# One layer on one core: experts' gate and up products with stationary weights, scatters without mutual order, and part of the experts' transfers on GpSimd's queue

## The chip, the core and the metric

The kernel runs on one core of a Trainium2 chip. The core has TensorE (PE) for matrix products, VectorE (DVE) and ScalarE (ACT) for elementwise work, GpSimd (POOL), and SyncE (SP), which issues most of the DMAs. Each engine executes its own instructions in order and waits on semaphores for the others. DMAs issued from SP and from POOL are carried by the same 16 DMA engines.

The metric is the device time of one execution in microseconds (us), here the median of several runs. Lower is better. Before the change it is 2605.57 us (three runs, 2600.91 to 2608.23).

## The reference

The layer takes 512 rows of width 512 (`x`) and a context of 8192 rows. It adds three blocks to `x` one after the other: cross attention with 16 heads of width 64, a state-space block with an MLP, and a mixture of 16 experts with a shared expert. The parts that the change touches are the projections at the start of the attention and the experts:

```python
x = x + _L0_xattn_ref(_layernorm(x), ctx, ctx, Wq, bq, Wk, bk, Wv, bv, Wo, bo)
...
logits = jnp.einsum('btc,ec->bte', x, router_w)          # x is the layernormed row
top_vals, top_idx = jax.lax.top_k(logits, 2)
gates = jax.nn.sigmoid(top_vals)
w_full = zeros((N, 16)).at[arange(N)[:, None], sel].add(gates)
gu = jnp.einsum('nc,ech->neh', xf, gate_up_w)            # 16 experts, 512 -> 2 x 512
gate, up = jnp.split(gu, 2, axis=-1)
h = jax.nn.silu(gate) * up
out_all = jnp.einsum('neh,ehc->nec', h, down_w)          # 512 -> 512
moe = jnp.einsum('ne,nec->nc', w_full, out_all)
shared = silu(x @ shared_gate.T) * (x @ shared_up.T) @ shared_down.T
x = x + moe + shared
```

Every row goes to its two best experts only, so the kernel gathers rows by expert.

## The kernel before

**Numbers in pairs.** All large products run in fp16 with a high and a low half of each operand and three matmuls per product (high by high, high by low, low by high), summed in fp32 in PSUM. A weight that comes from DRAM as fp32 is therefore split: ACT writes the high half, DVE the low half.

**Start (pass 0 of the attention).** `filler` (L426) is a generator that emits the key, value and query projections. For head pairs 0 and 1 it goes over 16 chunks of 512 context rows. For each chunk, `ctx_first` (L224) loads two pieces of 512 KB, splits them and stores the halves; `kproj_units` (L247) and `vproj_units` (L267) multiply them by the weights. `stage_w` (L168) loads a weight and `split_w` splits it; `load_w` does both at once. The staging tiles of Wk for pair 1 and of Wv share the tag `p32` and its three buffers with the context pieces `cf` (L229). `first_norm` (L186) normalises `x` and transposes it, `qproj` (L203) makes the queries; both are emitted after chunk 0 (L483 to L486). `smax_units` (L287) is the pass that finds each row's maximum: in pass 0 a unit is four matmuls into four PSUM banks (L300), four ACT copies (L305) and one DVE maximum. These units are queued in the list `side`, and `pump` (L429) hands one out after every fourth projection unit. PE's order in this part is the order in which `filler` emits, by hand; the other engines' order is set by the scheduler of the framework.

**Middle.** From about 250 us to 2230 us the attention's main loop and then the state-space block run. The change does not touch them.

**Experts (`tail`, L633).** Here the framework schedules all engines. The shared expert (`ffn`, L955, with the weights `rsg`, `rsu`, `rsd`) runs for the two halves of the rows. Its weights use the tag `wpm`, which has five buffers. Meanwhile DVE works out, for each row, the two slots (`sg`) in a table `xd_d` in DRAM, which holds 128 rows for each of 23 groups: 16 experts and 7 overflow groups. Eight indirect DMAs on POOL's queue scatter the rows into the table (L1199 to L1204), 128 rows of 2 KB each. The framework sees eight writes to one tensor and makes each wait for the one before.

Then `moe` (L1259) goes over 18 groups: 16 experts and 2 overflow groups. The other five run only in a branch that depends on a count. For each group k:

- `pieces` (L1084) loads four gate-and-up pieces and two down pieces of 512 KB each, in fp32, through the six buffers `wef` on SP's queue, and splits them: into `we` (18 buffers) and into `wpm` (the five that the shared expert uses too).
- `moe_in` (L1206) loads the group's rows `xd` from the table on SP's queue (three buffers), transposes them on PE in eight steps, and ACT copies the result to `xk`.
- `moe_up` (L1217) multiplies with the *rows* stationary: 24 matmuls, each with a 128x128 block of `xk` loaded into the array and 512 columns of weights moving. Row r of PSUM belongs to token r. ACT and DVE make silu(gate) times up and split it into `mgg`.
- `moe_turn` (L1237) transposes `mgg` on PE in eight steps so that features lie on partitions, and DVE copies the result to `mgT`. It is called in the middle of the *next* group's `moe_up`.
- `moe_down` (L1246) runs 12 matmuls with `mgT` stationary and 512 columns of the down weights moving. ACT copies the result to `myo`, and SP stores it to `y_d` (L1257).

At the end POOL gathers each row's two results from `y_d` (L1285), DVE adds them to `x_sb` with the gates (L1289), and SP stores the output.

Of the kernel before, what the change touches and what calls it, by code (L numbers as in the profile page):

```python
# [8 lines left out]
F16 = mybir.dt.float16  # L9
# [7 lines left out]
P = 128  # L17
# [7 lines left out]
WS = 16.0  # L25
# [13 lines left out]
def perceiver_layer(ctx: ExitStack, tc: tile.TileContext, a: dict, out: bass.AP):  # L39
# [120 lines left out]
    bq_sb = sb1.tile([P, NPAIR], F32, name="bq_sb")  # L160
    bk_sb = sb1.tile([P, NPAIR], F32, name="bk_sb")
    bv_sb = L.tile([P, NPAIR], F32, name="bv_sb")
    nc.sync.dma_start(bq_sb, a["bq"])
    nc.sync.dma_start(bk_sb, a["bk"])
    nc.sync.dma_start(bv_sb, a["bv"])
    nc.vector.tensor_scalar(bk_sb, bk_sb, WS, None, ALU.mult)

    def stage_w(src, n, tag, stage=("wst", 1), bufs=2):  # L168
        st = sb2.tile([P, NC4, n], F32, name=f"wst_{tag}", tag=stage[0], bufs=stage[1])
        nc.sync.dma_start(st, src)  # L170
        return lambda: split_w(st, n, tag, bufs)

# [7 lines left out]
    def load_w(*x, **k):  # L180
        return stage_w(*x, **k)()
# [244 lines left out]
    def filler():  # L426
        side = []

        def pump():  # L429
            while side:  # L430
                u = next(side[0], None)
                if u is not None:
                    yield u
                    break
                side.pop(0)

        def pass_weights(g):
            pr = (2 * g, 2 * g + 1)
            out = []
            for src, n, tag, bufs in (  # L440
                (a["Wk"][pr[0]], P, "k", 4), (a["Wk"][pr[1]], P, "k", 4), (a["Wv"][g], 256, "v", 2),
                (a["Wq"][pr[0]], P, "q", 2), (a["Wq"][pr[1]], P, "q", 2),
            ):
                w = stage_w(src, n, tag, bufs=bufs)
                yield None
                out.append(w())
            yield out[0:2], out[2], out[3:5]

        nw = None
        for g in range(NPASS):  # L450
            pr = (2 * g, 2 * g + 1)
            if g == 0:
                wk0 = load_w(a["Wk"][0], P, "k", bufs=4)
                nct = ctx_first(0)
                wk = [wk0, load_w(a["Wk"][1], P, "k", ("p32", 3), bufs=4)]
                wv = load_w(a["Wv"][0], 256, "v", ("p32", 3))
                nc.sync.dma_start(x_sb, a["x"])
                wq = [load_w(a["Wq"][p], P, "q", ("t2k", 4)) for p in pr]
            else:
                wk, wv, wq = nw  # L460
                qh = [qproj(p, w) for p, w in zip(pr, wq)]
                yield 2 * 2592
            runm = [None, None]
            ks = [[None] * NCH for _ in pr]
            for c in range(NCH):
                if c == NCH - 7 and g < NPASS - 1:
                    nws = pass_weights(g + 1)
                if c >= NCH - 7 and g < NPASS - 1:
                    nw = next(nws, None) or nw
                ct = nct  # L470
                nxt = g * NCH + c + 1
                if nxt < NPASS * NCH:
                    nct = ctx_first(nxt) if nxt < NCH else ctx_load(nxt % NCH)
                gens = [kproj_units(p, c, ct, wk[i], ks[i]) for i, p in enumerate(pr)]
                gens += [vproj_units(g, c, ct, wv, j) for j in range(2)]
                k = 0
                for n, gen in enumerate(gens):
                    for u in gen:
                        yield u
                        k += 1  # L480
                        if k % (2 if g else 4) == 0 or len(side) > 2:
                            yield from pump()
                if g == 0 and c == 0:  # L483
                    first_norm()
                    qh = [qproj(p, w) for p, w in zip(pr, wq)]
                    yield 2 * 2592  # L486
                if c == 2:
                    for p, q in zip(pr, qh):
                        qplace(p, *q)
                side += [smax_units(c, i, qh[i][0], ks[i][c], runm, g == 0) for i in range(2)]  # L490
            side += [maxrow_units(p, i, runm) for i, p in enumerate(pr)]
            if g == NPASS - 1:
                while side:
                    yield from pump()
                    yield LAST / 10
            passes[0] = g + 1
# [136 lines left out]
def tail(tc, a, out, const, scr, ident, x_sb, mlp_d, oT, y_d, xd_d, psums):  # L633
# [562 lines left out]
    oii = G.tile([P, NOV + 1], I32, name="oii")  # L1196
    nc.vector.tensor_copy(oii, oid)

    for i in range(4):  # L1199
        for j in range(2):  # L1200
            nc.gpsimd.indirect_dma_start(
                out=xd_d[:], out_offset=bass.IndirectOffsetOnAxis(ap=sg[:, j, i : i + 1], axis=0),
                in_=xf[:, i].rearrange("p x d -> p (x d)"), in_offset=None,
            )  # L1204

    def moe_in(k):  # L1206
        xd = g2.tile([P, 2, NC4, P], F16, name="xd", bufs=3)
        nc.sync.dma_start(xd, xd_d[k * P : (k + 1) * P, :].rearrange("t (x d m) -> t x d m", x=2, d=NC4))
        pt = bank_j([P, 2, NC4, P], F16, "pxd")
        for x in range(2):  # L1210
            for d in range(NC4):
                nc.tensor.transpose(pt[:, x, d, :], xd[:, x, d, :], id16)
        xk = g2.tile([P, 2, NC4, P], F16, name="xk", bufs=2)
        nc.scalar.copy(xk, pt)
        return xk

    def moe_up(xk, ws, mid):  # L1217
        pg = bank_j([P, 512], F32, "pmg")
        pu = bank_j([P, 512], F32, "pmu")
        for d in range(NC4):  # L1220
            if d == 2 and mid:
                mid()
            for n, (x, y) in enumerate(((0, 0), (0, 1), (1, 0))):
                for o, ps in ((0, pg), (512, pu)):
                    nc.tensor.matmul(
                        ps, lhsT=xk[:, x, d, :], rhs=ws[d][:, y, o : o + 512],
                        start=d == 0 and n == 0, stop=d == 3 and n == 2,
                    )
        g = F2.tile([P, 512], F32, name="mg", tag="g32", bufs=2)
        nc.scalar.activation(g, pg, AF.Silu, scale=IW)  # L1230
        nc.vector.scalar_tensor_tensor(g, pu, IW, g, ALU.mult, ALU.mult)
        gg = F2.tile([P, 2, 512], F16, name="mgg", tag="gg", bufs=2)
        nc.scalar.copy(gg[:, 0], g)
        nc.vector.tensor_tensor(gg[:, 1], g, gg[:, 0], ALU.subtract)
        return gg

    def moe_turn(gg):  # L1237
        pt = bank_j([P, 2, NC4, P], F16, "pmt")
        for x in range(2):
            for c in range(NC4):  # L1240
                nc.tensor.transpose(pt[:, x, c, :], gg[:, x, c * P : (c + 1) * P], id16)
        gT = g2.tile([P, 2, NC4, P], F16, name="mgT", bufs=2)
        nc.vector.tensor_copy(gT, pt)
        return gT

    def moe_down(k, gT, ws):  # L1246
        py = acc(k % 4)
        for c in range(NC4):
            for n, (x, y) in enumerate(((0, 0), (0, 1), (1, 0))):
                nc.tensor.matmul(  # L1250
                    py, lhsT=gT[:, x, c, :],
                    rhs=ws[4 + c // 2][:, y, (c % 2) * 512 : (c % 2) * 512 + 512],
                    start=c == 0 and n == 0, stop=c == 3 and n == 2,
                )
        yo = g2.tile([P, DM], F32, name="myo", tag="yo", bufs=4)
        nc.scalar.activation(yo, py, AF.Copy, scale=IW)
        nc.sync.dma_start(y_d[k * P : (k + 1) * P, :], yo)  # L1257

    def moe(ks, weights):  # L1259
        xk = moe_in(ks[0])  # L1260
        prev = None
        turned = []
        for k in ks:
            ws = weights(k)
            gg = moe_up(xk, ws, prev and (lambda: turned.append(moe_turn(prev[1]))))
            if k < ks[-1]:
                xk = moe_in(k + 1)
            if prev:
                moe_down(prev[0], turned.pop(), prev[2])
            prev = k, gg, ws  # L1270
        moe_down(prev[0], moe_turn(prev[1]), prev[2])

    regs = [nc.sync.value_load(oii[0:1, k : k + 1], min_val=0, max_val=15) for k in range(NOV)]
    for _ in rs0:
# [87 lines left out]
```

## Time and profile before

| what | us |
|---|---|
| median of three runs | 2605.57 |
| the profiled execution, its own time | 2611.01 |
| its span, first to last instruction | 2609.3 |
| PE busy / DVE busy / ACT busy / POOL busy | 2383.2 / 2062.4 / 1949.2 / 44.3 |

The profile is of one execution. Its span is 1.7 us shorter than its own time, and its time is 5.4 us above the median. A page of the profile gives, for the whole span, the busy time of each engine; further views give the busy time, the TensorE clock that was granted and the DMA rate for chosen stretches, the instructions in order of time, and for each wait the instruction that ended it. PE is busy for 91% of the span, but this is a mean over stages with different limits, and a matmul's recorded duration (380 ns for 512 columns) is longer than its distance to the next one (216 ns), because matmuls overlap.

Where the stages lie: pass 0 of the attention from 0 to about 250 us; main loop and state-space block to about 2230 us; the rest of the MLP and the first half of the shared expert to about 2352 us; the scatters from 2352.8 us to 2387 us, beside the shared expert's second half; 18 groups of experts from 2402 us to 2587 us; gathers and output to 2609 us.

### The profile page before, as it was taken

The numbers are of one execution on the slowest core, as the hardware profiler recorded it, in microseconds if no ns is written. First come the engines' busy times: TensorE is split into PE (matmuls) and PEld (weight loads), VectorE is DVE, ScalarE is ACT, GpSimd is POOL, SyncE is SP. The second block draws the span as 40 slices with busy tenths as digits, with TensorE's granted clock in tenths as the row PEclk, the third lists the DMA queues.
The fourth block names the chain that finished last, engine by engine and source line by source line (L and its number), as shares of the span: only waits on it lengthen the run. The fifth ranks groups of instructions, "written<-read, shape, count | busy, mean of one in ns | idle before, by whom it ended". The sixth has DMA issues, their size and how long they took to land. (4 is left out here: it accounts for less than half of the span.)

```text
span 2609.3 us, 54424 instructions
## 1 busy us (share of the span) xinstructions
PE 2383.2 (91%) x21806; PEld 1676.5 (64%) x21806; DVE 2062.4 (79%) x2403; ACT 1949.2 (75%) x3734; POOL 44.3 (2%) x58
## 2 busy tenths in 40 slices
PE   7999899999999999999999998997877688998895
PEld 3555577776677777767777777995665466665442
DVE  6776588888888888878888778997899999533785
ACT  5787788888788888868888888997776476333784
POOL 2000000000000000000000000000000000001001
PEclk9999999999999999999999999999989899999998
DMA  7974677778687778778877655877510222766896
GB/s 270 312 259 138 231 212 231 229 235 241 199 234 235 226 221 251 226 199 228 236 221 213 175 156 148 207 205 192 159 41 25 97 81 82 260 225 217 293 331 208
DMA packets 353688, 531.43 MB, mean 204 GB/s; under 512 B 25107, under 2 KB 218835, under 8 KB 353301
## 3 DMA queue, kind: packets, MB, share of 16 engines
q1 hardware_dynamic: 352148, 523.69, 65.8%
q0 software_dynamic: 1280, 4.20, 0.5%
q8 instruction: 173, 2.83, 0.5%
q14 instruction: 87, 0.70, 0.1%
HBM read 397.68 MB, written 126.94 MB: 201 GB/s over the span
## 5 line engine op out<-in xcount | busy, mean ns | idle before, releaser
L377 DVE TENSOR_TENSOR phl<-p,phl 128x1024 f16<-128x1024 f32 x512 | 626.7, 1225 | 193.2 <-ACT phl L374 181.0
L372 ACT ACTIVATE p<-pss 128x512 f32<-128x512 f32 x1024 | 597.7, 622 | 114.5 <-PE pss L365 42.2
L305 ACT ACTIVATE sf<-psx 128x512 f16<-128x512 f32 x1024 | 558.5, 625 | 70.9 <-PE psx L300 70.1
L364 PE MATMUL pss<-qhh,k 128*128 128x256 f16 x2048 | 481.0, 275 | 14.3 <-ACT phl L374 12.0
L365 PE MATMUL pss<-qlm,kb 128*128 128x256 f16 x2048 | 479.7, 274 | 0.9 <-DMA kb<-k_d 0.9
L313 DVE TENSOR_TENSOR runm<-runm,sf 128x2048 f16<-128x2048 f16 x240 | 292.3, 1219 | 51.7 <-ACT sf L305 51.5
L394 PE MATMUL po<-v,phl 128*128 128x130 f16 x4096 | 322.7, 220 | 3.9 <-DVE oq L407 3.4
L374 ACT ACTIVATE phl<-pss 128x512 f16<-128x512 f32 x512 | 312.8, 611 | 0.0
L394 PEld LDWEIGHTS <-phl 128*128 128x128 f16 x4096 | 271.0, 98 | 61.6 <-issue 14.8
L275 PE MATMUL psv<-wh_v,ctxc 128*128 128x256 f16 x1024 | 282.0, 275 | 7.3 <-ACT wh_v L176 3.2
L276 PE MATMUL psv<-wl_v,ctxc 128*128 128x256 f16 x1024 | 280.8, 274 | 1.2 <-DVE wl_v L177 1.2
L277 PE MATMUL psv<-wh_v,ctxc 128*128 128x256 f16 x1024 | 280.9, 274 | 0.0
L364 PEld LDWEIGHTS <-k 128*128 128x128 f16 x2048 | 200.9, 98 | 66.0 <-issue 20.0
L365 PEld LDWEIGHTS <-kb 128*128 128x128 f16 x2048 | 201.4, 98 | 53.0 <-issue 14.6
L300 PE MATMUL psx<-khl,qh 64*128 64x512 f16 x1024 | 208.9, 386 | 17.6 <-ACT sf L305 12.2
L922 PE MATMUL py<-hs,ident 128*128 128x256 f32 x512 | 144.0, 437 | 73.5 <-DVE hs L919 73.5
L397 PE MATMUL po<-v,phl 128*128 128x65 f16 x4096 | 208.5, 193 | 2.5 <-DVE phl L377 2.5
L251 PE MATMUL psk<-ctxc,wh_k 128*128 128x512 f16 x512 | 198.0, 387 | 9.9 <-ACT ctxc L234 8.1
L376 DVE CAST phl<-p 128x1024 f16<-128x1024 f32 x256 | 176.0, 687 | 32.2 <-ACT p L372 32.0
L252 PE MATMUL psk<-ctxc,wh_k 128*128 128x512 f16 x512 | 196.3, 383 | 0.8 <-DVE ctxc L235 0.7
L253 PE MATMUL psk<-ctxc,wl_k 128*128 128x512 f16 x512 | 196.3, 383 | 0.0
L922 PEld LDWEIGHTS py<-hs,ident 128*128 128x128 f32 x512 | 107.2, 217 | 107.0 <-DVE hs L919 87.0
(304 smaller groups left out, 3774.6 us busy)
## 6 DMA issues: line engine op xcount, KB each, us to landing
v<-v_d SPq DMA_DIRECT2D x128, 520.0 KB
k<-k_d SPq DMA_DIRECT2D x256, 256.0 KB
ctxc<-ctx_d SPq DMA_DIRECT2D x96, 512.0 KB
wef<-in_gu_dram SPq DMA_DIRECT2D x72, 512.0 KB
v_d<-vs SPq DMA_DIRECT2D x128, 260.0 KB
k_d<-khl SPq DMA_DIRECT2D x128, 256.0 KB
kb<-k_d SPq DMA_DIRECT2D x128, 256.0 KB
wpm<-w_d SPq DMA_DIRECT2D x48, 512.0 KB
```

The source lines that it names most:

```text
L275: nc.tensor.matmul(ps[:, t, :], lhsT=ct[i // 2][:, 0, i % 2, sl], rhs=wh[:, i, :], start=i == 0, stop=False)
L276: nc.tensor.matmul(ps[:, t, :], lhsT=ct[i // 2][:, 0, i % 2, sl], rhs=wl[:, i, :], start=False, stop=False)
L277: nc.tensor.matmul(ps[:, t, :], lhsT=ct[i // 2][:, 1, i % 2, sl], rhs=wh[:, i, :], start=False, stop=i == NC4 - 1)
L305: nc.scalar.activation(dst, ps, AF.Copy, scale=1.0 / (8.0 * WS))
L313: nc.vector.tensor_tensor(r, r, sf, ALU.max)
L364: nc.tensor.matmul(ps[:, hh], lhsT=k[:, hh, sl], rhs=qhh[:, hh, qs], start=True, stop=False)
L365: nc.tensor.matmul(ps[:, hh], lhsT=b[:, hh, sl], rhs=qlm[:, hh, qs], start=False, stop=True)
L372: nc.scalar.activation(p32[:, i], pss[i], AF.Exp, scale=sc)
L374: nc.scalar.activation(ph[:, i], pss[i], AF.Exp, scale=sc)
L377: nc.vector.tensor_tensor(pl, p32, ph, ALU.subtract)
L394: nc.tensor.matmul(o, lhsT=ph[:, i, hh, qs], rhs=vv, start=first, stop=False, **kw)
L922: nc.tensor.matmul(py[:, j, :], lhsT=ident, rhs=hs[:, n, 1:], start=k == 0, stop=False)
```

## The change

It has three parts.

**Start.** The three bias loads leave the head of SP's queue: `bk` is loaded behind Wk and Wv, `bq` and `bv` behind Wq. The staging tiles of Wk for pair 1, Wv and Wq take the buffers of the main loop's `k` and `v` tiles, which are idle at that time, and no longer share buffers with the context pieces. Chunk 1's context is loaded before chunk 0 is multiplied. `first_norm` and `qproj` are emitted after chunk 1 instead of after chunk 0. The maximum units of chunk 0 are queued there too, and then units are handed out one behind the other until only chunk 1's two generators are left.

**Scatters and queues.** The eight scatters are declared independent of each other. The loads of `xd` and the stores to `y_d` move from SP's queue to POOL's, and each load of `xd` is given a dependency on all eight scatters.

**Experts.** `moe_up` makes the *weights* stationary: for each block of the contraction and each of the three products, eight blocks of 128x128 weights are loaded one after the other and 128 columns of `xk` move past each. The result has features on partitions, so `moe_turn` with its eight transposes and its DVE copy is gone, and `moe_down` takes `mgg` as it is.

```diff
-    nc.sync.dma_start(bq_sb, a["bq"])
-    nc.sync.dma_start(bk_sb, a["bk"])
-    nc.sync.dma_start(bv_sb, a["bv"])
-    nc.vector.tensor_scalar(bk_sb, bk_sb, WS, None, ALU.mult)
...
-        st = sb2.tile([P, NC4, n], F32, name=f"wst_{tag}", tag=stage[0], bufs=stage[1])
+        pool = L if stage[0] in ("k", "v") else sb2
+        st = pool.tile([P, NC4, n], F32, name=f"wst_{tag}", tag=stage[0], bufs=stage[1])
...
-                wk = [wk0, load_w(a["Wk"][1], P, "k", ("p32", 3), bufs=4)]
-                wv = load_w(a["Wv"][0], 256, "v", ("p32", 3))
+                wk1, wv = stage_w(a["Wk"][1], P, "k", ("k", 2), bufs=4), stage_w(a["Wv"][0], 256, "v", ("k", 2))
+                nc.sync.dma_start(bk_sb, a["bk"])
+                nc.vector.tensor_scalar(bk_sb, bk_sb, WS, None, ALU.mult)
+                nxt0 = ctx_first(1)
+                wk, wv = [wk0, wk1()], wv()
                 nc.sync.dma_start(x_sb, a["x"])
-                wq = [load_w(a["Wq"][p], P, "q", ("t2k", 4)) for p in pr]
+                wq = [stage_w(a["Wq"][p], P, "q", ("v", 3)) for p in pr]
+                nc.sync.dma_start(bq_sb, a["bq"])
+                nc.sync.dma_start(bv_sb, a["bv"])
...
-                if g == 0 and c == 0:
+                if g == 0 and c == 1:
                     first_norm()
-                    qh = [qproj(p, w) for p, w in zip(pr, wq)]
+                    qh = [qproj(p, w()) for p, w in zip(pr, wq)]
                     yield 2 * 2592
+                    side += [smax_units(0, i, qh[i][0], ks[i][0], runm, True) for i in range(2)]
...
-                side += [smax_units(c, i, qh[i][0], ks[i][c], runm, g == 0) for i in range(2)]
+                if g or c:
+                    side += [smax_units(c, i, qh[i][0], ks[i][c], runm, g == 0) for i in range(2)]
+                if (g, c) == (0, 1):
+                    while len(side) > 2:
+                        yield from pump()
...
+            for o in sent:
+                tc.declare_no_dep(d.ins, o.ins, reason="every slot is one token's: the rows differ")
+            sent.append(d)
...
-        nc.sync.dma_start(xd, xd_d[k * P : (k + 1) * P, :].rearrange("t (x d m) -> t x d m", x=2, d=NC4))
+        r = nc.gpsimd.dma_start(xd, xd_d[k * P : (k + 1) * P, :].rearrange("t (x d m) -> t x d m", x=2, d=NC4))
+        for o in sent:
+            tc.add_manual_dep(
+                r.ins, o.ins.name, mybir.DependencyInfo(mybir.DependencyClass.Sync, mybir.DependencyReason.DATA),
+                reason="rows of every scatter",
+            )
...
-            for n, (x, y) in enumerate(((0, 0), (0, 1), (1, 0))):
+            for n, (x, y) in enumerate(((0, 0), (1, 0), (0, 1))):
                 for o, ps in ((0, pg), (512, pu)):
-                    nc.tensor.matmul(
-                        ps, lhsT=xk[:, x, d, :], rhs=ws[d][:, y, o : o + 512],
-                        start=d == 0 and n == 0, stop=d == 3 and n == 2,
-                    )
+                    for c in range(NC4):
+                        nc.tensor.matmul(
+                            ps[:, c], lhsT=ws[d][:, y, o + c * P : o + (c + 1) * P], rhs=xk[:, x, d, :],
+                            start=d == 0 and n == 0 and c == 0, stop=d == 3 and n == 2, skip_group_check=True,
+                        )
...
-    def moe_turn(gg):
-        pt = bank_j([P, 2, NC4, P], F16, "pmt")
...
-        nc.sync.dma_start(y_d[k * P : (k + 1) * P, :], yo)
+        nc.gpsimd.dma_start(y_d[k * P : (k + 1) * P, :], yo)
...
-            gg = moe_up(xk, ws, prev and (lambda: turned.append(moe_turn(prev[1]))))
+            gg = moe_up(xk, ws)
             if k < ks[-1]:
                 xk = moe_in(k + 1)
             if prev:
-                moe_down(prev[0], turned.pop(), prev[2])
+                moe_down(*prev)
```

More of the change, by code (lines that the diff above doesn't have):

```diff
@@ L471, in filler @@
                 nxt = g * NCH + c + 1
-                if nxt < NPASS * NCH:
+                if nxt == 1:
+                    nct = nxt0
+                elif nxt < NPASS * NCH:
                     nct = ctx_first(nxt) if nxt < NCH else ctx_load(nxt % NCH)
@@ L1197, in tail @@
     nc.vector.tensor_copy(oii, oid)
+    sent = []
     for i in range(4):
         for j in range(2):
-            nc.gpsimd.indirect_dma_start(
+            d = nc.gpsimd.indirect_dma_start(
                 out=xd_d[:], out_offset=bass.IndirectOffsetOnAxis(ap=sg[:, j, i : i + 1], axis=0),
@@ L1215, in moe_in, with moe_up @@
         return xk
-    def moe_up(xk, ws, mid):
-        pg = bank_j([P, 512], F32, "pmg")
-        pu = bank_j([P, 512], F32, "pmu")
+    def moe_up(xk, ws):
+        pg = bank_j([P, NC4, P], F32, "pmg")
+        pu = bank_j([P, NC4, P], F32, "pmu")
         for d in range(NC4):
-            if d == 2 and mid:
-                mid()
-            for n, (x, y) in enumerate(((0, 0), (0, 1), (1, 0))):
+            for n, (x, y) in enumerate(((0, 0), (1, 0), (0, 1))):
                 for o, ps in ((0, pg), (512, pu)):
-                    nc.tensor.matmul(
-                        ps, lhsT=xk[:, x, d, :], rhs=ws[d][:, y, o : o + 512],
-                        start=d == 0 and n == 0, stop=d == 3 and n == 2,
-                    )
-        g = F2.tile([P, 512], F32, name="mg", tag="g32", bufs=2)
+                    for c in range(NC4):
[3 more added lines that the diff above has]
+                        )
+        g = F2.tile([P, NC4, P], F32, name="mg", tag="g32", bufs=2)
         nc.scalar.activation(g, pg, AF.Silu, scale=IW)
         nc.vector.scalar_tensor_tensor(g, pu, IW, g, ALU.mult, ALU.mult)
-        gg = F2.tile([P, 2, 512], F16, name="mgg", tag="gg", bufs=2)
+        gg = F2.tile([P, 2, NC4, P], F16, name="mgg", tag="gg", bufs=2)
         nc.scalar.copy(gg[:, 0], g)
@@ L1235, in moe_up @@
         return gg
-    def moe_turn(gg):
-        pt = bank_j([P, 2, NC4, P], F16, "pmt")
[L1239 to L1244, printed above, removed]
     def moe_down(k, gT, ws):
@@ L1261, in moe @@
         prev = None
-        turned = []
         for k in ks:
             ws = weights(k)
-            gg = moe_up(xk, ws, prev and (lambda: turned.append(moe_turn(prev[1]))))
+            gg = moe_up(xk, ws)
             if k < ks[-1]:
@@ L1268, in moe @@
             if prev:
-                moe_down(prev[0], turned.pop(), prev[2])
+                moe_down(*prev)
             prev = k, gg, ws
-        moe_down(prev[0], moe_turn(prev[1]), prev[2])
+        moe_down(*prev)
     regs = [nc.sync.value_load(oii[0:1, k : k + 1], min_val=0, max_val=15) for k in range(NOV)]
```

## The prediction

> **What bounds the kernel now.** I read the busy shares by stage first, because 91% for PE over the span says nothing about the stages that the change touches. Columns: stretch, its length, busy us (instructions) of PE, PEld, DVE, ACT, POOL, granted clock, DMA share, GB/s.
>
> ```profile
> 2303.00:2380.00 77.00, 73.89 (x583) 52.69 (x581) 25.64 (x68) 21.03 (x30) 5.94 (x6) 1.00 0.60 202
> 2380.00:2397.00 17.00, 8.21 (x50) 5.02 (x48) 4.97 (x5) 4.07 (x6) 1.91 (x2) 0.80 0.57 202
> 2397.00:2467.00 70.00, 60.20 (x338) 30.02 (x336) 51.09 (x53) 49.36 (x59) 0.00 (x0) 0.95 0.81 278
> 2467.00:2567.00 100.00, 95.09 (x562) 46.42 (x559) 84.28 (x87) 78.99 (x97) 0.00 (x0) 1.00 0.91 331
> ```
>
> Just ahead of the experts there is a hole: from 2380 to 2397 us every engine is idle half the time or more. Then come 70 us in which no unit is full, then 100 us in which PE and DMA nearly are. The issues of POOL and SP in order of time (start, length) say what the hole is:
>
> ```profile
> 2352.83 1.15 POOL L1201 DMA_INDIRECT xd_d<-xf,sg  x1 [135.70 <-DVE sg L1184]
> 2356.02 0.97 POOL L1201 DMA_INDIRECT xd_d<-xf,sg  x1 [2.04 <-DMA xd_d<-xf,sg]
> 2362.56 0.96 POOL L1201 DMA_INDIRECT xd_d<-xf,sg  x1 [5.57 <-DMA xd_d<-xf,sg]
> ...
> 2384.12 0.95 POOL L1201 DMA_INDIRECT xd_d<-xf,sg  x1 [2.01 <-DMA xd_d<-xf,sg]
> ...
> 2387.22 1.31 SPq L1208 DMA_DIRECT2D xd<-xd_d  x3
> 2388.64 0.37 SPq L761 DMA_DIRECT2D wpm<-rsu_d  x1
> ```
>
> Each scatter waits for the one before, so eight take 34 us. Three loads of `xd` stand at the head of SP's queue until the last has landed, and behind them stands `rsu`, the shared expert's last weight, which does not need the scatters at all. The waits from 2385 us on (total, times, longest) price this, and show that SP is held up in every group as well:
>
> ```profile
> PE pu L703 <- DMA wpm<-rsu_d: 8.8, 1, 8.8
> ...
> SPq L1257 <- ACT myo L1256: 73.0, 18, 9.2
> SPq L1208 <- DMA xd_d<-xf,sg: 14.5, 1, 14.5
> ```
>
> The store of `y_d` holds SP for 73.0 us in all; weight loads queue behind it.
>
> **Head of the experts.** Undone: the order among scatters, and SP's wait. POOL needs 0.95 us for one scatter and 0.3 us to the next issue (the gathers at the end run at that pace: 0.98 at 2591.14, the next at 2592.43). Eight are issued by 2352.8 + 8 x 1.26 = 2362.9 us and landed by about 2367 us (a scatter lands in 3.8 us), not 2387. The `xd` loads then have over 15 us until PE wants them. PE's first half of the last shared step ends at 2385.7 us; the 24 matmuls of its second half need 24 x 0.109 = 2.6 us at full clock, so they end at 2388.3 us instead of 2399.6 us (after the wait they also ran at half clock). That is 11.3 us, and the first group need not wait for `xk` again (0.7 us more). I take **-12 us**. Bounds: eight scatters (2 MB) at once share the DMA engines with the shared expert's weights, 202 GB/s there; if that delays a weight by 4 us the gain is 8 us; at best 13.3 us.
>
> **Group by group.** Before, the first gate matmul is at 2402.35 us and the last up matmul ends at 2575.95 us: 173.6 / 18 = 9.64 us per group. On PE the change takes away 24 matmuls of 512 columns and 8 transposes, and adds 96 matmuls of 128 columns. What costs most if wrong is the distance between two matmuls of 128 columns when each brings new weights. Two places show it:
>
> ```profile
> 1000.35 0.62 PE L394 MATMUL po<-v,phl 128*128 128x130 f16 x8
> 1000.81 0.40 PE L397 MATMUL po<-v,phl 128*128 128x65 f16 x8
> ...
> 2413.58 0.61 PE L1241 MATMUL pmt<-id,mgg 128*128 128x128 f16 x8
> 2414.03 0.38 PE L1225 MATMUL pmg<-we,xk 128*128 128x512 f16 x1
> ```
>
> Eight attention matmuls of 130 columns, each with its own 128x128 weights, take 0.46 us (57 ns each); the next eight, of 65 columns, 0.33 us (41 ns). Eight transposes take 0.45 us (56 ns). So a weight load costs at most 41 ns and hides behind 128 columns. Against the change speaks the Trainium skill, "TensorE: Matmul & The Clock Gate", Back-to-back issue gap: a sustained stream of weight load and matmul pairs runs at about 81 ns per matmul with 128 columns and 131 ns with 512. By that rule a group's matmuls go from 24 x 131 + 16 x 81 + 12 x 131 ns = 6.0 us to 96 x 81 + 8 x 81 + 12 x 131 ns = 10.0 us, 72 us more in 18 groups. The trace contradicts both figures (56 and 216 ns), and its rows are of the very same form, so I take the rows: from 24 x 216 + 16 x 56 + 12 x 216 ns = 8.67 us to 104 x 56 + 12 x 216 ns = 8.42 us.
>
> The rest of 9.64 us is waiting: from 2396 us on PE's waits add up to 19.8 us, 1.1 per group, mostly for `xk`, for `we` and for the drain of `pmg`. Part goes: DVE loses the 0.685 us copy of `mgT`, PE the wait for `mgT` and `mgg` (3.3 us in all), and SP no longer stops, so ACT's 30.3 us of waiting for `wef` shrinks. Late next are three units at once: ACT (six splits of 1.06, `xk` 1.01, three copies of 0.6: 9.2 us as recorded, about 8.2 back to back), DVE (8.0), and the DMAs. Of 108 weight pieces 18 are in before the hole; 90 x 0.524 MB, 15 `xd` and 18 stores of 0.262 MB are 55.8 MB. They can resume when `wpm` buffers come free, about 2384 us, not 2389.6. At the 331 GB/s of the late row this is 169 us, to 2553 us; at 368 GB/s, the best 10 us here, 152 us. A group needs between 8.6 us (PE nearly bare) and 10.0 us (new queue order hurts); I take 9.1, which ends at nearly the time that 331 GB/s allows: 18 x (9.1 - 9.64) = **-9.7 us** (bounds -18.7 and +6.5).
>
> **POOL's queue.** POOL gets 36 more issues, 18 loads and 18 stores, at about 1.26 us (the nearest row, the gathers): 2.5 us of a 9 us group, on an engine with 0.00 busy there. A store waits for `myo`, and behind it stands the next `xd`; three buffers leave that load a whole group's time. The skill, "SBUF — State Buffer", section "SBUF: two separate sides", warns that GpSimd cannot write its DMA descriptors while DVE runs an operation that uses both its port pairs. If each issue waited for one DVE split (1.22 us), POOL would need 5 us per group: still hidden. Nor do DVE's rows here run at doubled pace: 1.22 us per 1024 elements, where the attention's cast of 1024 takes 0.69. Cost nothing; if an `xd` were late each time, its 2 to 3 us would go to PE.
>
> **The end.** After the last up matmul it takes 10.6 us to the last store (2586.6 us). The turn goes: down products began at 2581.76, the first half of `mgg` was there at 2579.4, the second at 2580.5, so about 2 us less; POOL's issue is 0.6 us longer than SP's 0.33. **-1.5 us** (-2.3 to +1). The 22.7 us of gathers stay.
>
> **The start.**
>
> ```profile
> 20.36 0.27 PE L275 MATMUL psv<-wh_v,ctxc 128*128 128x256 f16 x1 [3.24 <-ACT wh_v L176]
> 21.80 0.37 PE L276 MATMUL psv<-wl_v,ctxc 128*128 128x256 f16 x1 [1.17 <-DVE wl_v L177]
> ...
> 50.95 1.80 PE L300 MATMUL psx<-khl,qh 64*128 64x512 f16 x4
> ```
>
> Wv waits for a `p32` buffer, so PE idles 4.4 us and runs the next 4.2 us at half clock (2.1 lost). The biases hold Wk back by 1.4 us. Gain: 7.9 us. Against it: after chunk 1 the maximum units run one behind the other. Chunk 0's two generators hold four units and the loop hands out one more. Each needs four ACT copies (2.05 us) for 0.54 us of PE; the third row shows a unit close behind another taking 1.80 us. Four waits of 1.5 us are 6 us. Net **-2 us** (-8 if later stalls of this kind shrink, +5 if chunk 1's context is late, for DMA is at 0.76 to 0.97 in the first 80 us).
>
> **Sum.** -12 - 9.7 - 1.5 - 2 = -25.2 us. The profiled execution, 2611.0 us of its own (span 2609.3), would become 2585.8; it lies 5.4 us above the median shown, and from 2605.6 the forecast is **2580 us**. Its own range, 2563 to 2596: all favourable bounds give -42, and no gain at all in the groups -15, plus the start's +5.
>
> **Rivals.** (a) *DMA keeps its old mean pace*: from 2389.6 to 2576 us it moved 56.4 MB, 303 GB/s. If SP's waits were not what kept it there, loads gain only the earlier resumption, 5.6 us; with start and end -9, **2597 us**. For it: a DMA share of 0.91. Against: 368 GB/s while SP still stopped in each group. (b) *The head stays*: the `wpm` buffers or the crowded scatters hold the shared expert, 10 of the 12 us are lost: **2591 us**. The schedule is free here, so the change may not do what it says. (c) *Weight loads set PE's pace*: at 81 ns a group takes 104 x 81 + 12 x 216 ns = 11.0 us, so 18 x 1.4 = +24.5, less 15.5 elsewhere: +9, **2615 us**, slower. It decides from 76 ns on, where the group reaches 10.5 us. Against it stand the 56 and 57 ns above; for it, that 96 in a row are a longer stream than any eight.
>
> **Numbers.** Forecast 0.64, (a) 0.14, (b) 0.10, (c) 0.12. A measurement of this kernel tells some 0.3%, 8 us, from nothing. Forecast, (b) nearly whole and half of (a) are faster: 0.79; within 0.3% 0.09; slower, (c), 0.12. The range that leaves out (c) and a little else: 2563 to 2603.
>
> **What would show it.** Scatters 1.3 us apart; `rsu` issued before 2370 us, no hole at 2385; gate matmuls 56 ns apart; SP without waits on `myo`; groups at 9.1 us with DMA at 330 GB/s or more; Wv's wait gone and five maximum units in a row near 40 us. Gate matmuls at 76 ns or more, or PE waiting for `xd`, would make it wrong.

## The result, and the profile after

The changed kernel takes **2617.48 us** (median of 12 runs, 2611.31 to 2620.38), the kernel before 2607.05 us in the same comparison (12 runs, 2600.85 to 2612.6). The ratio is 1.0042 with a 95% interval of 1.0032 to 1.0051: some 10 us slower, where 25 us less were forecast. The profiled execution of the changed kernel took 2615.82 us (span 2613.7), 4.8 us more than the profiled one before. Of the two profiled executions, that before lies 4.0 us above its median and that after 1.7 us below, so laid out along landmarks the two spans differ by 4.4 us only:

| stretch of the profiled executions, us | before | after | difference | forecast |
|---|---|---|---|---|
| start of the span to the first scatter | 2352.8 | 2355.7 | +2.9 | -2 |
| first scatter to the first gate matmul | 49.5 | 41.8 | -7.7 | -12 |
| first gate to last up matmul, 18 groups | 173.8 | 184.8 | **+11.0** | -9.7 |
| last up matmul to the end | 33.2 | 31.4 | -1.8 | -1.5 |

The third row is off by 20.7 us, with the wrong sign. The first has the wrong sign too, but its 2.9 us say little: in the traces of the ten kernels here that have the old start, the first scatter stands anywhere from 2351.4 to 2359.0 us. The busy times of the changed kernel by stage (columns as in the prediction: stretch, length, busy us of PE, PEld, DVE, ACT, POOL, granted clock, DMA share, GB/s):

```profile
2380.00:2397.00 17.00, 15.61 (x117) 10.80 (x118) 7.28 (x9) 7.63 (x10) 0.54 (x1) 1.00 0.49 165
2397.00:2467.00 70.00, 59.50 (x797) 50.20 (x796) 47.86 (x49) 46.81 (x57) 5.95 (x11) 0.95 0.82 283
2467.00:2567.00 100.00, 82.97 (x1062) 66.10 (x1060) 78.03 (x75) 77.69 (x93) 9.20 (x17) 0.98 0.94 339
2567.00:2591.00 24.00, 19.26 (x236) 14.62 (x235) 8.68 (x10) 10.17 (x15) 2.16 (x4) 1.00 0.15 58
```

The last of these stretches in the kernel before:

```profile
2567.00:2591.00 24.00, 13.56 (x64) 5.88 (x64) 10.48 (x12) 9.33 (x12) 0.00 (x0) 0.87 0.32 106
```

The hole ahead of the experts is closed: PE is busy for 15.61 us of the first row instead of 8.21. But in the third row PE has 12 us more idle time than before while the DMAs move a little more, and in the fourth PE works on for 19 us, 6 more than before, while the DMAs are nearly done (share 0.15). Weights had arrived that PE could not use until the loads were over.

The issues of POOL and SP in order of time (start, length, idle time and what ended it):

```profile
2355.68 1.15 POOL L1211 DMA_INDIRECT xd_d<-xf,sg  x1 [138.23 <-DVE sg L1193]
2357.13 0.97 POOL L1211 DMA_INDIRECT xd_d<-xf,sg  x1 [0.30 <-issue]
...
2364.73 0.96 POOL L1211 DMA_INDIRECT xd_d<-xf,sg  x1 [0.30 <-issue]
...
2382.79 0.32 SPq L770 DMA_DIRECT2D wpm<-rsu_d  x1
...
2388.96 0.33 SPq L1098 DMA_DIRECT2D wef<-in_gu_dram  x1
```

The scatters are 1.27 us apart, as forecast, and the last load of `rsu` no longer waits for them: it is issued at 2382.8 us instead of 2388.6. That is still not before 2370, as the prediction had it, because SP stops there for PE to free `wpm` buffers (17.6 us behind `acc` in four stops from 2345 us on). The experts' weights resume at 2389.0 us, not at 2384.

The matmuls of one group, on PE's timeline:

```profile
2486.53 0.39 PE L1243 MATMUL pmu<-xk,we 128*128 128x128 f16 x4
2486.75 0.39 PE L1243 MATMUL pmg<-xk,we 128*128 128x128 f16 x4
2486.97 0.39 PE L1243 MATMUL pmu<-xk,we 128*128 128x128 f16 x4
2487.20 0.61 PE L1230 MATMUL pxd<-id,xd 128*128 128x128 f16 x8
2487.64 2.75 PE L1259 MATMUL acc<-wpm,mgg 128*128 128x512 f16 x12
2491.86 0.38 PE L1243 MATMUL pmg<-xk,we 128*128 128x128 f16 x4 [1.47 <-ACT xk L1232]
```

Four matmuls, each with its own weights, start every 0.22 us: 56 ns each, in a run of 96. Rival (c), 81 ns, is out. What PE waits for is in the last line: `xk`, for which the transposes had been done since 2487.8 us. ACT's timeline says why it came so late:

```profile
2485.10 1.06 ACT L1103 ACTIVATE we<-wef 128x1024 f16<-128x1024 f32 x1 [1.48 <-DMA wef<-in_gu_dram]
2486.06 0.58 ACT L1265 ACTIVATE myo<-acc 128x512 f32<-128x512 f32 x1
2486.54 1.05 ACT L1103 ACTIVATE wpm<-wef 128x1024 f16<-128x1024 f32 x1
2487.49 2.94 ACT L1103 ACTIVATE we<-wef 128x1024 f16<-128x1024 f32 x3
2490.33 0.58 ACT L1248 ACTIVATE mg<-pmg 128x512 f32<-128x512 f32 x1
2490.81 1.01 ACT L1232 COPY xk<-pxd 128x1024 f16<-128x1024 f16 x1
```

Four splits stand ahead of `mg` and `xk`, and another had just waited 1.48 us for its transfer. Three of the four are pieces of the group after the one that `xk` starts. ACT goes through its list in order, so whatever one split waits for, `xk` waits for too. (The Trainium skill, "PSUM — Partial Sum Buffer", section "Engine vs sequencer instructions", states it as a rule: ScalarE, VectorE and GpSimd take their queues strictly first in, first out. The timeline above agrees: `xk` could have run from 2487.8 us and starts at 2490.81, when the splits are done.) The waits from 2385 us on (total, times, longest):

```profile
ACT we L1103 <- DMA wef<-in_gu_dram: 31.9, 26, 4.5
...
PE pmg L1243 <- ACT xk L1232: 21.2, 13, 3.2
```

ACT's wait for `wef` was 30.3 us before and did not shrink; PE's wait for `xk` was 4.1 us, and 8.4 in `stat_only` below, which has the same matmuls in the old order.

**A number for the order.** Call L(k) the number of weight pieces that ACT has split when it copies `xk` of group k, less 6k, the pieces of the groups before k; it is counted along ACT's instructions in each trace. L says how many of the coming pieces must have landed and been split before PE may start group k. Its gate and up products need four; whatever L has above that is weights which PE does not want yet. The framework chose this order when it built each kernel; nothing in the code states it.

- before: 17 15 13 12 10 9 9 9 7 7 5 5 4 3 2 1 0 0
- after: 17 16 13 12 11 10 9 9 9 9 9 9 9 9 9 9 9 5

Before, L falls by about one per group to nothing: each group waits for five new pieces and uses up one that was loaded ahead. After, L stays at 9. Then each group waits for six new pieces, one whole group's worth, and its pace is that of the transfers: between 2467 and 2567 us nine stores left, one every 10.7 us on average, and 10.7 us at 339 GB/s are 3.6 MB, about one group's six pieces of 0.524 MB, one `xd` and one store (3.67 MB).

### The profile page after: what moved, and what is told of

It reads as the page before. It is cut to its first block, busy times and chain, and to the rows that moved or that the text cites. A ratio compares the mean times of both kernels' runs of the same rounds, so it can differ in the third digit from the quotient of the medians.

```text
span 2613.7 us, 56729 instructions
## 1 busy us (share of the span) xinstructions
PE 2381.6 (91%) x22958; PEld 1729.3 (66%) x22958; DVE 2051.3 (78%) x2385; ACT 1948.6 (75%) x3734; POOL 62.8 (2%) x94
```

## The experiments

The theory, called order theory: ACT's order with a constant L ties PE to the weights' arrivals. Its rivals: the queue theory (POOL's transfers and the weights' buffers set the pace), the form theory (stationary weights cost the time) and the start theory (the start's part holds the whole loss). All results are against runs of the kernel before on the same chip; "groups" is first gate to last up matmul in the profiled run (before: 173.8, after: 184.8).

| kernel | median us | ratio to before, 95% | groups us | last six L |
|---|---|---|---|---|
| start_only | 2610.44 | 1.0004 to 1.0028 | 171.4 | 4 3 2 1 0 0 |
| scat_queues | 2609.67 | 1.0003 to 1.0022 | 181.4 | 9 9 8 8 8 5 |
| stat_only | 2604.60 | 0.9989 to 1.0005 | 170.0 | 5 4 3 2 1 0 |
| no_start | 2615.94 | 1.0024 to 1.0051 | 187.5 | 9 9 9 9 9 5 |
| no_start_ysp | 2603.59 | 0.9984 to 1.0002 | 180.4 | 7 6 5 5 5 5 |
| no_start_sp | 2601.40 | 0.9970 to 0.9986 | 170.3 | 5 4 3 2 1 0 |
| lead_as_before | 2585.73 | 0.9913 to 0.9943 | 158.5 | 4 3 2 1 0 0 |
| half_same_order | 2585.43 | 0.9899 to 0.9936 | 156.9 | 8 8 8 8 8 5 |
| lead_sp | 2596.55 | 0.9939 to 0.9967 | 169.3 | 3 2 1 0 0 0 |
| lead_rows | 2596.68 | 0.9937 to 0.9965 | 167.5 | 4 3 2 1 0 0 |
| lead_full | 2590.16 | 0.9908 to 0.9939 | 160.6 | 4 3 2 1 0 0 |
| lead_full_spread | 2585.45 | 0.9900 to 0.9925 | 159.4 | 4 3 2 1 0 0 |

The runs were made in three groups, each on one chip; the medians of the kernel before in them lie between 2606.2 and 2608.2 us; kernels that did not run together are compared by median and by ratio. "Groups" is from one profiled execution each. Kernels that differ in the start alone differ there by 2 to 3 us (173.8 and 171.4; 184.8 and 187.5; 158.5 and 160.6), so a smaller difference says nothing.

**The parts, one at a time.** `start_only` has the start part of the change alone:

```diff
+                nxt0 = ctx_first(1)
...
-                if g == 0 and c == 0:
+                if g == 0 and c == 1:
                     first_norm()
```

> The kernel before with the start part of the change alone. Queue theory (the groups are paced by the weights' transfers and by the buffers that hold them; the start loses some 3 us, the store from POOL's queue some 2 us, the groups what the head gains): the first main-loop matmul comes 3 to 6 us later and the time is +3 us (+1 to +6). Start theory (the rows of the start hold the whole loss): +10 us. Form theory (weight-stationary matmuls cost the loss): 0 to +3 us.

+4.2 us (+1 to +7), as the queue theory had it. The first main-loop matmul stands at 298.2 us, 7.0 us later than before (3 to 6 were expected); but in the ten kernels with the old start it stands anywhere from 290.8 to 297.4 us.

`scat_queues` has the scatters without order and POOL's queue, with rows stationary and the old start:

```diff
+                tc.declare_no_dep(d.ins, o.ins, reason="every slot is one token's: the rows differ")
...
+        r = nc.gpsimd.dma_start(xd, xd_d[k * P : (k + 1) * P, :].rearrange("t (x d m) -> t x d m", x=2, d=NC4))
...
+        nc.gpsimd.dma_start(y_d[k * P : (k + 1) * P, :], yo)
```

> The kernel before with the scatters without order and with xd and y_d on POOL's queue; rows stay stationary, the start is the old one. Queue theory: the first expert matmul comes some 8 us earlier after the first scatter, the groups give most of it back because the weights' loads start no earlier and run at an unchanged pace, the end loses 2 us: 0 us (-4 to +4). Form theory: the head's gain is kept, -8 to -12 us. Start theory: -8 us or better.

+3.4 us (+1 to +6): the head gained 9.6 us (49.5 to 39.9), the groups lost 7.6. So the groups give back most of the head's gain with the *old* matmuls too, and L is 8 or 9 almost to the end. PE waits here less for `xk` than for `mg`, the copy that empties a PSUM bank for the transposes and that stands on ACT behind the same splits; this kernel, then the kernel before:

```profile
PE pxd L1221 <- ACT mg L1239: 13.0, 8, 2.8
PE pmg L1234 <- ACT xk L1223: 4.6, 6, 1.5
```

```profile
PE pxd L1212 <- ACT mg L1230: 6.3, 3, 4.2
PE pmg L1225 <- ACT xk L1214: 4.1, 5, 1.4
```

`stat_only` has the stationary weights alone:

```diff
+                            ps[:, c], lhsT=ws[d][:, y, o + c * P : o + (c + 1) * P], rhs=xk[:, x, d, :],
```

> The kernel before with the weights stationary alone; scatters, queues and start are the old ones. Queue theory: PE's work per group falls a little, the weights' transfers keep the pace: 0 us (-4 to +3), groups near 9.6 us. Form theory: the groups go from 9.6 us to 10.3 us or more, +10 to +15 us, with the first expert matmul where it was.

-0.8 us (-3 to +1): the form alone costs nothing, and its groups are 3.8 us shorter. The form theory as stated falls here.

`no_start` is the changed kernel with the old start.

```diff
-                nxt0 = ctx_first(1)
...
-                if g == 0 and c == 1:
+                if g == 0 and c == 0:
                     first_norm()
```

> The changed kernel with the old start. Queue theory: 3 us (1 to 6) below the changed kernel, so +4 to +9 us against before. Start theory: equal to before or faster. Form theory: at the changed kernel's time, +8 to +12 us.

+9.9 us (+6 to +13), above the upper end of what the queue theory gave it. The start theory falls. The form theory had given just this; that stationary weights might hurt only where the scatters are out of the way stays possible until `no_start_sp` and `lead_rows` below. The parts do not add up, either: +3.4 and -0.8 alone, +9.9 together. Together L is 9 to the end, the largest of all. That sent me to ACT's order; the following runs start from `no_start`.

**ACT's order.** `lead_as_before` prescribes nothing but the order in which ACT is given its work: each split of a weight piece is told to stand behind the `xk` copy that has the falling L of the kernel before. DVE's splits, which need ACT's halves, follow.

```diff
+    LEAD = (17, 15, 13, 12, 10, 9, 9, 9, 7, 7, 5, 5, 4, 3, 2, 1, 0, 0)
...
+                due = [q for q in range(min(len(xks), 18)) if 6 * q + LEAD[q] <= nsp[0] < 108]
+                if due:
+                    tc.add_manual_dep(
+                        h.ins, xks[due[-1]].ins.name,
+                        mybir.DependencyInfo(mybir.DependencyClass.NoSync, mybir.DependencyReason.DATA),
...
-        nc.scalar.copy(xk, pt)
+        xks.append(nc.scalar.copy(xk, pt))
```

> The changed kernel with the old start; ACT's order alone is pinned: the copy xk of group k stands before the split of weight piece 6k+L, L falling from 17 to 0 over the 18 groups as in the kernel before (in the changed kernel L stays at 9). Order theory (ACT runs in order, so with a constant L each group's xk waits for a weight piece that lands in the same group, PE keeps the DMAs' pace and the stock of three groups loaded ahead is used up only after the loads have ended): first gate to last up matmul falls from 187 to 165-172 us, time 2596 to 2604 us, 12 to 20 us below the changed kernel with the old start (2615.9). Queue theory (POOL's transfers and the weights' buffers set the pace whatever the order): 2611 to 2618 us.

2585.73 us: 19 us below before (ratio 0.9928) and 29 us below `no_start` by the ratios (1.0038 less 0.9928, whose intervals lie far apart), more than the theory gave it. The groups take 158.5 us, 8.8 us each, instead of 187.5. Busy times by stage and waits, in `no_start` and then in `lead_as_before`:

```profile
2397.00:2467.00 70.00, 58.13 (x753) 48.30 (x751) 47.79 (x47) 47.46 (x58) 6.48 (x12) 0.93 0.83 280
2467.00:2550.00 83.00, 71.79 (x912) 58.97 (x910) 62.88 (x60) 62.85 (x76) 8.11 (x15) 0.94 0.95 336
```

```profile
ACT we L1094 <- DMA wef<-in_gu_dram: 34.4, 24, 3.9
PE pmg L1234 <- ACT xk L1223: 17.7, 11, 3.3
```

```profile
2397.00:2467.00 70.00, 64.80 (x901) 53.80 (x898) 54.51 (x54) 54.65 (x67) 7.56 (x14) 1.00 0.91 326
2467.00:2550.00 83.00, 79.93 (x1099) 65.63 (x1097) 72.09 (x70) 73.14 (x89) 8.66 (x16) 1.00 0.99 369
```

```profile
ACT we L1097 <- DMA wef<-in_gu_dram: 9.8, 11, 1.7
PE pmg L1245 <- ACT xk L1234: 6.7, 6, 2.3
```

On ACT:

```profile
2497.85 2.94 ACT L1097 ACTIVATE we<-wef 128x1024 f16<-128x1024 f32 x3
2500.69 0.58 ACT L1250 ACTIVATE mg<-pmg 128x512 f32<-128x512 f32 x1
2501.17 1.01 ACT L1234 COPY xk<-pxd 128x1024 f16<-128x1024 f16 x1
```

The splits still stand right ahead of `mg` and `xk`, but now of pieces that have landed. PE is busy 96% of the second row (79.93 of 83) instead of 86%, and the DMAs move 369 GB/s instead of 336: with PE no longer held back, the loads run faster too. ACT's wait for `wef` falls from 34.4 us to 9.8. POOL's queue and the six `wef` buffers are as they were, so the queue theory falls. One caution: the order as built is a little tighter than the list asks (16 14 10 9 9 8 at the beginning), and PE's own order changes in the first three and the last two groups. Between the fourth and the fifteenth store, where PE's order is the same in both kernels, a group takes 8.9 us instead of 10.7, so the gain is not confined to the ends. ACT's order and DVE's were not changed apart from each other; PE's longest waits in `no_start` are for ACT.

`no_start_ysp` puts only the stores back on SP's queue, `no_start_sp` the loads of `xd` too:

```diff
-        nc.gpsimd.dma_start(y_d[k * P : (k + 1) * P, :], yo)
+        nc.sync.dma_start(y_d[k * P : (k + 1) * P, :], yo)
```

> The changed kernel with the old start and the stores of y_d back on SP's queue. ACT's order as built has L falling from 17 to 5 only. Order theory: between the two, first gate to last up matmul 175 to 182 us, and 1 to 2 us less between last store and first gather: 2603 to 2610 us. Queue theory (what POOL carries costs): the same direction, since half of POOL's transfers go; so this run tells little between the two by itself.

> The changed kernel with the old start, stores of y_d and loads of xd both on SP's queue; scatters without order and stationary weights stay. ACT's order as built has L falling from 17 to 0. Order theory: first gate to last up matmul 168 to 174 us as before, head kept: 2594 to 2601 us. Form theory (stationary weights only hurt once the scatters are out of the way): 2610 us or more.

`no_start_ysp` gives 2603.59 us with L ending at 5, `no_start_sp` 2601.40 us with L ending at 0; groups 180.4 and 170.3 us. The groups are as the order theory has it; the second time is 0.4 us above its range. Nor did `no_start_sp` take the 2610 us or more that the form theory gave it. The two runs also show what the constant L goes with: the fewer transfers stand between the weight loads on SP's queue, the further ahead the framework puts the splits on ACT (with both on SP's queue L falls to 0, with the stores alone to 5, with neither it stays at 9). Why it does so is not on record.

`half_same_order` pins the order of `no_start` (as built L is 8 instead of 9) and leaves out half of the weights' transfers. The piece before is split a second time in their place, so ACT, DVE and PE keep their work:

```diff
+                if k % 2 == 0:
+                    f = g2.tile([P, 1024], F32, name="wef", bufs=6)
+                    nc.sync.dma_start(f, src(t, slice(k * 1024, k * 1024 + 1024)))
```

> The changed kernel with the old start and its constant L (8 to 9), but every second weight piece is not loaded: the piece before it is split a second time, so half of the experts' weight bytes and their products are left out. Order theory (groups wait for weights that are landing): groups fall from 10.8 us to 8.5-9.2 us, first gate to last up matmul near 160 us, time 2583 to 2592 us. Queue theory with POOL's own latencies as the pace: groups stay above 10.3 us, 2608 us or more.

2585.43 us, groups 156.9 us, in the steady part 9.2 to 9.3 us each. Its busy times in 90 us of the groups and its wait:

```profile
2467.00:2557.00 90.00, 84.72 (x1144) 69.05 (x1141) 74.56 (x73) 73.90 (x92) 8.66 (x16) 1.00 0.53 174
```

```profile
PE pmg L1246 <- ACT xk L1235: 1.1, 1, 1.1
```

With nearly the same order and half of the bytes PE's wait for `xk` is gone (17.7 us in `no_start`). So the order costs time only through the weights that are still landing; POOL, PE and the six splits per group fit into 9.3 us.

**With the order pinned, what is each part worth?** `lead_sp` is `lead_as_before` with `xd` and `y_d` on SP's queue, `lead_rows` is `lead_as_before` with the rows stationary.

```diff
-        r = nc.gpsimd.dma_start(xd,
+        r = nc.sync.dma_start(xd,
...
-        nc.gpsimd.dma_start(y_d[
+        nc.sync.dma_start(y_d[
```

> The kernel lead_as_before (2585.7 us) with the stores of y_d and the loads of xd on SP's queue; ACT's order is pinned to the same falling L. If SP's stops behind the stores cost weight transfers, as the prediction said: first gate to last up matmul 166 to 171 us instead of 158.5, time 2594 to 2602 us, as in no_start_sp. If no_start_sp was slow through its order alone: 2584 to 2589 us.

2596.55 us, more than on POOL's queue by 10.8 us in the medians, by 6.5 in the ratios (0.9953 and 0.9928); the groups take 10.8 us more. SP's longest wait in this run:

```profile
SPq L1268 <- ACT myo L1267: 76.8, 17, 7.3
```

So SP's stops behind the stores do cost transfers, as the prediction held; the DMAs moved 337 GB/s from 2467 to 2550 us, against 369. `no_start_sp` has the same queues and an L that is larger above all in the first five groups. It is slower by 4.9 us in the medians and 6.5 in the ratios, but its groups differ by 1.0 us only (170.3 and 169.3): the tighter beginning is not what shortened the groups by 29 us, and where the rest of the 5 to 6.5 us lies is not shown.

```diff
+            xk = moe_in(ks[0])
...
+            gg = moe_up(xk, ws, prev and (lambda: turned.append(moe_turn(prev[1]))))
```

> The kernel lead_as_before with the rows stationary again (transposes and the copy of mgT back); scatters, queues and the pinned order are the same. If PE and DVE near the floor set the groups now: the form is worth 0.3 to 0.7 us per group, so 5 to 12 us more, 2591 to 2598 us. If the weights' transfers set them: 2585 to 2588 us.

2596.68 us: the stationary form is worth 11 us by the medians, 6 by the ratios. The groups differ by 9.0 us (167.5 against 158.5), and from the last up matmul to the last store it takes 9.0 us instead of 6.6.

**The start.** `lead_full` is the changed kernel complete, with the order pinned. `lead_full_spread` leaves out the loop that hands out chunk 0's maximum units one behind the other:

```diff
-                if (g, c) == (0, 1):
-                    while len(side) > 2:
-                        yield from pump()
```

> The whole changed kernel, start part included, with ACT's order pinned (L from 17 to 0). Order theory: all of the loss beyond the start was the order, so 28 to 32 us below the changed kernel plus what the start part costs: 2586 to 2592 us, the first main-loop matmul at 297 us against 293.5 us. If the start part costs nothing, as the changed kernel with and without it suggests (10.4 and 9.9 us over before): 2584 to 2587 us.

> lead_full without the loop that hands out chunk 0's maximum units one behind the other after chunk 1: they go out one after each projection unit of chunk 2 instead. If the five units in a row are what the start part loses (20 matmuls took 9.2 us from 48.4 us on, 4.3 us at full pace, and PE's clock was halved behind them): the first main-loop matmul 4 to 7 us earlier than in lead_full, time 4 to 7 us lower. If the wait of the transposes of x for DVE (4.6 us before 41 us, half clock behind it) is the loss: 0 to 2 us lower.

2590.16 and 2585.45 us on one chip. Against `lead_as_before` the start part costs 4.4 us by the medians and nothing by the ratios (0.9924 and 0.9928). Spreading the units wins 4.7 us by the medians, 2.9 by the ratios, whose intervals overlap: the times point to the five units and do not settle it. The first main-loop matmul stands at 295.4 and 290.5 us (291.2 before, with the spread given above). PE's timeline in the changed kernel, and its busy times from 40 to 60 us, then those before:

```profile
39.06 1.11 PE L100 MATMUL pt_x<-ident,xn 128*128 128x128 f32 x4 [3.98 <-DVE vs L279]
...
48.41 0.61 PE L297 MATMUL psx<-khl,qh 64*128 64x512 f16 x4
49.74 7.92 PE L297 MATMUL psx<-khl,qh 64*128 64x512 f16 x16 [0.73 <-ACT sf L302]
```

```profile
40.00:60.00 20.00, 18.23 (x55) 6.07 (x55) 11.31 (x17) 13.27 (x25) 5.88 (x5) 0.67 0.70 220
```

```profile
40.00:60.00 20.00, 18.60 (x111) 8.83 (x110) 11.85 (x15) 15.61 (x31) 0.00 (x0) 1.00 0.77 259
```

PE counts as busy, but it runs 55 matmuls in 20 us at a granted clock of 0.67, before the change 111 at 1.00. The twenty matmuls of the five units take 9.2 us (48.4 to 57.6), 4.3 at 0.216 each. In the spread version each unit is followed by projections, which run at 0.22 us each:

```profile
50.67 1.62 PE L297 MATMUL psx<-khl,qh 64*128 64x512 f16 x4
52.22 0.39 PE L248 MATMUL psk<-ctxc,wh_k 128*128 128x512 f16 x1
```

Both `lead_as_before` and `lead_full_spread` beat the kernel before and the changed one by far more than their intervals; between the two the runs do not decide.

## Why the prediction was wrong

**The step that failed** is "Group by group", and in it the sentence that with SP no longer stopped "ACT's 30.3 us of waiting for `wef` shrinks", from which 9.1 us per group followed. It counted the work of each engine and took the order of that work on ACT as given. The order was made anew by the build: L stayed at 9. The wait was 31.9 us, the groups took 10.3 us on average (184.8 / 18) and 10.7 in the steady part, more than the 10.0 that were the bound for "new queue order hurts". That the framework is free here was named in rival (b), but only for the head. Slower was expected from rival (c) alone, at 0.12, and neither sign named for being wrong, gate matmuls at 76 ns or PE waiting for `xd`, came up. With the order pinned the groups take 8.8 to 8.9 us (158.5 and 160.6 over 18), a little under the 9.1 that were forecast, and ACT's wait does shrink, to 9.8 us in `lead_as_before` (at 369 GB/s, though, where 9.1 had been worked out from 331). The complete change then comes to 2590.16 us, inside the range given.

**The range was too narrow by its own bounds.** The four unfavourable ones, -8, +6.5, +1 and +5, sum to +4.5, 2610 us, and the range ended at 2603 (the measured median lies above both); its 2596 leaves out the groups' and the head's bounds, and takes +5 for the start on top of the -2 already counted.

**Head: mechanism right, gain too large.** -7.7 us in the profile of the changed kernel, against -12 with a gain of 8 as the lower bound; in the kernels with an order pinned -7.5 to -9.8. The term that was too small is the crowding of the scatters: one landed after 7.1 us in the median (at most 7.3), before after 3.8. While they landed PE waited 2.1 us for `rsg`, which it had not done before, and behind that ran at a granted clock of 0.66 from 2368 to 2373 us, with the DMAs at a share of 0.94. It was taken as a bound and not as the value.

**Weights resume** 33.3 us after the first scatter (2389.0), not 31 (2384 after 2352.8), and the last was issued at 2564.0 us, where the transfers should have ended at 2553. In `lead_as_before` they were issued from 2385.6 to 2544.4 us, 159 us, less than the 169 that were worked out at 331 GB/s. Rival (a), the DMAs' old pace, was wrong as a cause: with only the order changed the loads rose from 336 to 369 GB/s.

**Stationary weights: right.** 56 ns per matmul; alone nothing in time (-0.8 us), and 6 to 11 us with SP's queue free and the order pinned.

**POOL's queue: right about its own cost, blind to its side effect.** A direct transfer keeps POOL for 0.54 us, less than the 1.26 assumed, and PE never waits for `xd`. But moving these transfers is what changed the order on ACT (`scat_queues`, `no_start_sp`).

**End: right in sum by luck.** -1.8 us against -1.5: the last store came 4.4 us sooner after the last up matmul (10.5 to 6.1), and the first gather 2.1 us later after the store.

**Start: no gain shown.** +4.2 us (+1 to +7) in `start_only`, inside the bounds of -8 and +5; the profile's +2.9 is within the spread of that landmark. The five units cost 4.9 us (9.2 less 4.3), about the 6 that were taken. Not foreseen were the transposes of `x`, which now wait 4.6 us for DVE, and the low granted clock behind both: 0.54 from 40 to 45 us, 0.50 from 55 to 60. What the start part costs in the complete kernel stays open: between the changed kernel and `no_start` it is 0.7 us by the medians and 1.0 by the ratios, each of which has an interval of 2 to 4 us either side.

## What to carry to other kernels

Where a framework orders the engines, moving a DMA to another queue can reorder an engine that issues none of them: count, before and after, how far ahead of the consumer's copies the producer's work stands on each in-order engine. A stock of data loaded ahead is worth something only if that distance falls over the loop; if it is constant, the consumer keeps the transfers' pace and the stock is used up after they have ended. When parts of a change do not add up, compare orders before durations.

## What the runs showed of the hardware

- 96 matmuls of 128 columns, each with its own 128x128 weights, kept 56 ns apart, the same as the eight in a row before the change.
- An issue of a direct transfer kept POOL for 0.54 us, that of an indirect one for 0.96 us.
- The DMAs moved 369 GB/s over 83 us at a share of 0.99, with PE at 96%, DVE at 87% and ACT at 88% busy.
- From the last store's issue to the first gather it took 3.8 to 7.1 us; on POOL's queue both 4.7 (`lead_as_before`) and 6.7 us (the changed kernel) occur, so the queue alone does not decide. In the five traces that tell when that store landed, it did so after 2.3 to 4.3 us (2.3 and 4.3 in these two), and the gather began 2.4 to 2.5 us later: what varies is the landing. Why was not tried.
